# A fused attention block and 7x7 convolution: the stage on v put in a fixed order of thirds, with the edge rows first

## The chip, the core and the metric

The kernel runs on one core of one Trainium2 chip. The metric is the device time of one execution in microseconds, taken as the median of the runs. The core has five engines that run beside each other and wait for one another by semaphores: TensorE (PE, matrix products into PSUM), VectorE (DVE), ScalarE (ACT), GpSimd (POOL) and SyncE (SP, here an issuer of DMAs). ACT, POOL and SP issue DMAs. All data is float32.

## What is computed

Two layers with a residual each, on x of 1 x 384 x 192 x 192. The first is a group norm, a 1x1 convolution to q, k and v, a 2x2 max pool, a 3x3 depthwise convolution, channel attention in 8 heads of 48 channels (four top-k softmaxes, mixed), gelu, doubling to the old size, and a 1x1 projection. The second is a group norm and a 7x7 depthwise convolution with a symmetrised kernel.

```python
# layer 0
qkv = einsum('bchw,oc->bohw', gn(x), w_qkv) + b_qkv
qkv = qkv.reshape(b, 3*c, hs, 2, ws, 2).max(axis=(3, 5))          # 2x2 max pool
qkv = depthwise3x3(qkv, w_dw) + b_dw
q, k, v = split(qkv, 3, axis=1)                                   # each (b, 8, 48, hs*ws)
attn = einsum('bhcn,bhdn->bhcd', unit(q), unit(k)) * temperature  # channel attention
out = sum(topk_softmax(attn, kk) @ v * a for kk, a in ((24, a1), (32, a2), (36, a3), (38, a4)))
out = gelu(out); out = repeat(repeat(out, 2, axis=2), 2, axis=3)
x = x + einsum('bchw,oc->bohw', out, w_proj) + b_proj
# layer 1
w_sym = (w + rot90(w, 1) + rot90(w, 2) + rot90(w, 3)) / 4
x = x + depthwise7x7(gn(x), w_sym)
```

The attention matrix needs q and k of the whole image, and the second group norm needs the whole sum of layer 0. So there are stages: the statistics of x; q and k; the attention matrix; v with attention, projection and residual; and the 7x7 convolution. The sum of layer 0 goes through DRAM (`sd`, and `sh` for the rows that neighbouring strips need) and is read again by the 7x7 stage.

## The kernel before

The 192 image rows are seen as 6 strips of 32 rows (`NT`, `TR`). A block takes the same two rows from each strip, so there are 16 blocks (`NBC`), worked in the order `FIRST, FIRST + 1, ...` modulo 16. Pooling makes one row per strip of a block. Channels are three tiles of 128 (`KT`). A depthwise row needs the pooled rows of the block before, its own and the next; the first two row sets are kept, the others rotate through three.

```python
FIRST = 3
...
    xp2 = dx.enter_context(tc.tile_pool(name="xp2", bufs=4))
    vp = dx.enter_context(tc.tile_pool(name="vp", bufs=5))
    pv = psx.enter_context(tc.tile_pool(name="pv", bufs=2, space=PSUM))
    # the attention matrix: one piece of program, ahead of everything on v
    ...
    for mt in range(KT):                       # rank of every entry among the 48 of its row
        nc.vector.tensor_tensor(gt, other, mine, ALU.is_gt)        # 128 x 2304 each
        nc.vector.tensor_tensor(eq, other, mine, ALU.is_equal)
        nc.vector.tensor_tensor(eq, eq, lower, ALU.mult)
        nc.vector.tensor_tensor(gt, gt, eq, ALU.add)
        nc.vector.tensor_reduce(rank[:, mt, :], gt, AX.X, ALU.add)
    ...
    gp = dx.enter_context(tc.tile_pool(name="gp", bufs=2))
    yp = dx.enter_context(tc.tile_pool(name="yp", bufs=3))
    xrp = dx.enter_context(tc.tile_pool(name="xrp", bufs=2))

    def convolve(i):                           # v before pooling: one block in three thirds
        for t0 in range(0, NT, UT):
            xb = xp2.tile([P, KT, UT, RB * HW], F32, tag="xv")
            for kt in range(KT):
                nc.sync.dma_start(xb[:, kt], image_rows(kt, b, t0, UT))
            for ct in range(KT):
                ps = pv.tile([P, UT, 512], F32, tag="pv")
                # 6 products: ps <- wq, xb                         (L677)
                nc.vector.tensor_reduce(rows[ct][...], ps[...], AX.XY, ALU.max)   # L681

    def depthwise_v(i):                        # 9 taps for each of three channel tiles, L467/L469
        for ct in range(KT):
            taps(vp.tile(...), 2 * KT + ct, win)

    def attend(i, vb):
        for ct in range(KT):
            for h in range(2):
                # 2 or 3 products: ps <- attnT, vb[dt]             (L712)
                nc.scalar.activation(gl[...], ps[:, 0:H], AF.Gelu) # L718

    def project(i, gl):
        for ot in range(KT):
            for h in range(2):
                # 3 products: ps <- wp, gl                         (L731)
                nc.scalar.activation(yh[:, h], ps[:, 0:H], AF.Identity, bias=..., accum_out=ysum[...])
            xr = xrp.tile([P, NT, RB * HW], F32, tag="xr")
            nc.sync.dma_start(xr, image_rows(ot, b, 0, NT))
            for e in range(CP):                # residual add, one column in four at a time, L756
                nc.vector.tensor_tensor(sx[:, v, :, :, dj : dj + NJ], xq[:, :, :, :, e], y[...], ALU.add)
            # two Square activations with accum_out, of 3/4 and 1/4 of sx (L769)
            for a in range(RB):
                nc.gpsimd.dma_start(sdv[r, cs], rows_of(a, CP, 0))            # L783
                # for r < 3 or r >= 29: three more DMAs into sh (halo rows)   # L793

    for i in range(NBC + 3):
        if i - 2 in vbs:  gls[i - 2] = attend(i - 2, vbs.pop(i - 2))
        if i < NBC:       convolve(i)
        if i - 2 in gls:  project(i - 2, gls.pop(i - 2))
        if 0 < i - 1 <= NBC:  vbs[i - 1] = depthwise_v(i - 1)
    ...
    # 7x7 stage: 48 steps of 8 channels; each loads w, main, aux on ACT's queue
    ws = {n: load_w(n) for n in range(2)}
    mains = {n: load_main(n) for n in range(2)}        # main <- sd, aux <- sh
    # group statistics, then rows of mean, std, 1/std over all 384 channels
    for name, v in (("mb", mean1), ("sb", std1), ("rb", rstd1)): along_free(t, v, mps, name)
    for k in range(5): nc.vector.tensor_scalar_mul(mm[:, :, k], mb, mask[:, k : k + 1])
    for n in range(steps): ...                         # 24 products (L1020, L1025, L1031), scaling, stores
```

The scheduler that builds the program may reorder instructions on an engine. `keep_in_program_order` (`keep`) takes this from it; before, only the 7x7 stage used it.

Of the kernel before, what the change touches and what calls it, by code (L numbers as in the profile page):

```python
# [73 lines left out]
FIRST = 3  # L74
# [4 lines left out]
def conv_preact_d2(  # L79
# [169 lines left out]
    st = const.tile([P, KT, NB * SUB, 6], F32, name="st0")  # L249
    mean0 = const.tile([P, KT], F32, name="mean0")  # L250
    rstd0 = const.tile([P, KT], F32, name="rstd0")
    with tc.tile_pool(name="gps0", bufs=1, space=PSUM) as gps:
# [287 lines left out]
    dx = bctx  # L540
    xp2 = dx.enter_context(tc.tile_pool(name="xp2", bufs=4))
    rowp2 = dx.enter_context(tc.tile_pool(name="rowp2", bufs=1))
    vp = dx.enter_context(tc.tile_pool(name="vp", bufs=5))
    pv = psx.enter_context(tc.tile_pool(name="pv", bufs=2, space=PSUM))
    near = {}
    with ExitStack() as ax:
        ap = ax.enter_context(tc.tile_pool(name="ap", bufs=1))
# [4 lines left out]
        nc.vector.reciprocal(rn, rn)  # L552
        tps = ptr.tile([P, C], F32, name="tps", tag="tr")
# [6 lines left out]
        along_free(rkb, rn[:, KT : 2 * KT], ptr, "rk", "tr")  # L560

# [7 lines left out]
        for i, (mt, r0, r1, h) in enumerate(PIECES):  # L569
            eng = (nc.gpsimd, nc.scalar)[i % 2]  # L570
            o = h * HC - SPAN[mt][0]
            eng.dma_start(att[r0:r1, mt, :], scaled[r0:r1, mt, o : o + HC])

# [8 lines left out]
        for mt in range(KT):  # L582
            full = [P, HC, HC]
            other = att[:, mt, :].unsqueeze(1).to_broadcast(full)
            mine = att[:, mt, :].unsqueeze(2).to_broadcast(full)
            gt = ap.tile(full, F32, name=f"gt{mt}", tag="gt")
            eq = ap.tile(full, F32, name=f"eq{mt}", tag="eq")
            nc.vector.tensor_tensor(gt, other, mine, ALU.is_gt)
            nc.vector.tensor_tensor(eq, other, mine, ALU.is_equal)
            nc.vector.tensor_tensor(eq, eq, lower, ALU.mult)  # L590
            nc.vector.tensor_tensor(gt, gt, eq, ALU.add)
            nc.vector.tensor_reduce(rank[:, mt, :], gt, AX.X, ALU.add)

# [5 lines left out]
        nc.scalar.activation(ex, ex, AF.Exp)  # L599
        mix = ap.tile(row3, F32, name="mix")  # L600
        for i, kk in enumerate(KKS):
# [9 lines left out]
            else:  # L611
                nc.vector.tensor_tensor(em, em, rsb, ALU.mult)
                nc.vector.tensor_tensor(mix, mix, em, ALU.add)
        diag = ap.tile([P, KT, C], F32, name="diag")
        nc.gpsimd.memset(diag, 0.0)
        for i, (mt, r0, r1, h) in enumerate(PIECES):
            eng = (nc.gpsimd, nc.scalar)[i % 2]
            eng.dma_start(diag[r0:r1, mt, h * HC : (h + 1) * HC], mix[r0:r1, mt, :])
        for dt in range(KT):
# [13 lines left out]
    bpm = const.tile([P, KT], F32, name="bpm")  # L633
    nc.vector.tensor_tensor(bpm, bp, mean0, ALU.subtract)
    ysum = const.tile([P, KT, NBC, 2], F32, name="ysum")
    sqsum = const.tile([P, KT, NBC, 2], F32, name="sqsum")
    mid1 = const.tile([P, KT], F32, name="mid1")
    negmid = const.tile([P, KT], F32, name="negmid")
    gp = dx.enter_context(tc.tile_pool(name="gp", bufs=2))
    yp = dx.enter_context(tc.tile_pool(name="yp", bufs=3))  # L640
    xrp = dx.enter_context(tc.tile_pool(name="xrp", bufs=2))
    sxp = dx.enter_context(tc.tile_pool(name="sxp", bufs=1))
# [3 lines left out]
    sxs = []  # L646
    for i in range(3):
        t = sxp.tile([P, LEAD + CP * RB * RUN + LEAD], F32, name=f"sx{i}")
        nc.gpsimd.memset(t, 0.0)
        sxs.append(t)  # L650
    H = PBC // 2
    order = [(FIRST + i) % NBC for i in range(NBC)]

# [12 lines left out]
    def convolve(i):  # L666
        b, rows = order[i], place(i)
        for t0 in range(0, NT, UT):
            xb = xp2.tile([P, KT, UT, RB * HW], F32, name=f"xv{b}_{t0}", tag="xv")
            for kt in range(KT):  # L670
                nc.sync.dma_start(xb[:, kt], image_rows(kt, b, t0, UT))
            for ct in range(KT):
                o = (2 * KT + ct) * P
                ps = pv.tile([P, UT, 512], F32, name=f"pv{b}_{t0}_{ct}", tag="pv")
                for u in range(UT):
                    for kt in range(KT):
# [4 lines left out]
                nc.vector.tensor_reduce(  # L681
                    rows[ct][:, 1 + t0 : 1 + t0 + UT, 1 : PS + 1],
                    ps[:, :, 0 : RB * HW].rearrange("p u (a w b) -> p u w a b", a=2, b=2),
                    AX.XY,
                    ALU.max,
                )

    def depthwise_v(i):

        b = order[i % NBC]  # L690
        vb = []
        for ct in range(KT):
            dst = vp.tile([P, NT, PS], F32, name=f"vb{b}_{ct}", tag="vb")

            def win(dy, dx):
                r = b + dy - 1
                t0 = 1 + r // NBC
                return place(i + dy - 1)[ct][:, t0 : t0 + NT, dx : dx + PS]

            taps(dst, 2 * KT + ct, win)  # L700
            vb.append(dst)
        return vb

    def attend(i, vb):
        b = order[i % NBC]
        gl = gp.tile([P, KT, PBC], F32, name=f"gl{b}", tag="gl")
        for ct in range(KT):
            dts = [dt for dt in range(KT) if ct in near[dt]]
            for h in range(2):
                ps = ptr.tile([P, C], F32, name=f"po{b}_{ct}_{h}", tag="tr")  # L710
                for dt in dts:
                    nc.tensor.matmul(  # L712
                        ps[:, 0:H],
                        attnT[:, dt, ct * P : (ct + 1) * P],
                        vb[dt].rearrange("p t c -> p (t c)")[:, h * H : (h + 1) * H],
                        start=(dt == dts[0]), stop=(dt == dts[-1]),
# [6 lines left out]
    def project(i, gl):  # L723
        b = order[i % NBC]
        for ot in range(KT):
            y = yp.tile([P, NT, NJ, 2], F32, name=f"y{b}_{ot}", tag="y")
            yh = y.rearrange("p (h t) j e -> p h (t j e)", h=2)
            for h in range(2):
                ps = ptr.tile([P, C], F32, name=f"pr{b}_{ot}_{h}", tag="tr")
                for ct in range(KT):  # L730
                    nc.tensor.matmul(  # L731
                        ps[:, 0:H],
                        wp[:, ct, ot * P : (ot + 1) * P],
                        gl[:, ct, h * H : (h + 1) * H],
                        start=(ct == 0), stop=(ct == KT - 1),
# [12 lines left out]
            xr = xrp.tile([P, NT, RB * HW], F32, name=f"xr{b}_{ot}", tag="xr")  # L748
            nc.sync.dma_start(xr, image_rows(ot, b, 0, NT))
            flat = sxs[(i * KT + ot) % len(sxs)]  # L750
            body = flat[:, LEAD : LEAD + CP * RB * RUN]
            sx = body.rearrange("p (v a t j) -> p v a t j", v=CP, a=RB, t=NT)
            xq = xr.rearrange("p t (a j e) -> p a t j e", a=RB, e=CP)
            for e in range(CP):
                v, dj = (e + CP - 1) % CP, int(e > 0)
                nc.vector.tensor_tensor(  # L756
                    sx[:, v, :, :, dj : dj + NJ],
                    xq[:, :, :, :, e],
                    y[:, :, :, e // 2].unsqueeze(1).to_broadcast([P, RB, NT, NJ]),
                    ALU.add,  # L760
                )
            runs = body.rearrange("p (n j) -> p n j", j=JP)
            for k, (n0, n1, dj) in enumerate(
                ((0, (CP - 1) * RB * NT, 1), ((CP - 1) * RB * NT, CP * RB * NT, 0))
            ):
                junk = yp.tile(
# [339 lines left out]
```

## Time and profile before

| | before |
|---|---|
| median of 3 runs | 3046.9 us (3043.93 to 3054.62) |
| profiled span | 3052.5 us |
| PE busy | 2697.0 us (88%) |
| DVE busy | 2309.6 us (76%) |
| ACT busy, POOL busy | 787.3 us, 757.3 us |
| DMA | 608.48 MB, mean 199 GB/s |
| first `pv` product (L677) | 1405.4 us |
| first `po` product (L712) | 1551.6 us |
| last `pv` product | 2268.0 us |
| first 7x7 product (L1020) | 2411.6 us |

The costly groups of the stage on v, from the list of groups; the columns are the line, the engine, the operation, what it writes from what, the sizes, the count, then busy time with the mean of one, and the idle time of the engine just before them with what ended most of it:

```profile
L677 PE MATMUL pv<-xv,wq 128*128 128x384 f32 x1728 | 575.2, 493 | 27.0 <-DVE row L681 25.3
L469 DVE SCALAR_TENSOR_TENSOR vb<-row,wd,vb 128x576 f32<-128x576 f32 x384 | 293.1, 811 | 2.1
L681 DVE TENSOR_REDUCE row<-pv 128x192 f32<-128x768 f32 x144 | 137.6, 955 | 187.0 <-PE pv L677 187.0
L756 DVE TENSOR_TENSOR sx<-xr,y 128x576 f32<-128x576 f32 x192 | 218.0, 1200 | 61.5 <-DMA xr<-in_x_dram 54.1
L712 PE MATMUL po<-vb,attnT 128*128 128x288 f32 x448 | 140.7, 456 | 49.7 <-ACT y L737 19.4
```

Durations of neighbours overlap on an engine, because instructions are pipelined. So the time that a group takes is better read from the starts of its instructions than from the sum of their durations.

### The profile page before, as it was taken

To read this page: it belongs to the slowest core of one execution; us is meant where nothing else is said; L and a number is where in the kernel's file an instruction comes from. 1 tells how busy PE (TensorE), PEld (TensorE's weight loads), DVE (VectorE), ACT (ScalarE), POOL (GpSimd) and SP (SyncE) were. 2 spreads that over 40 slices of the span, in tenths; PEclk is the share of its full clock that TensorE was granted. 3 is DMA by queue.
4 is the path that set the end of the run, shared out by engine and by line. 5 is a ranking of instruction groups with operands and counts; after the bars stand their busy time and mean duration, and the time that the engine had idled before them with its cause. 6 is when DMAs were issued, how large, how long until landed. Compare 5 with 4: busy or idle time off the path is not lost.

```text
span 3052.5 us, 25172 instructions
## 1 busy us (share of the span) xinstructions
PE 2697.0 (88%) x8661; PEld 1597.7 (52%) x8661; DVE 2309.6 (76%) x3350; ACT 787.3 (26%) x1497; POOL 757.3 (25%) x878
## 2 busy tenths in 40 slices
PE   0089999999999999999799999999996599989997
PEld 0044444444444444445465555555554477767675
DVE  7957787878787878787867687677677577867775
ACT  0011111111111111112003122122123355666664
POOL 0033444200000000001001000000133367776765
PEclk9999999999999999999999999999997699999999
DMA  9956676401010101002226556556689899999997
GB/s 370 415 179 234 229 243 224 145 31 62 31 62 32 62 31 62 31 1 91 98 93 226 183 170 229 167 187 220 220 265 361 313 345 348 362 362 350 354 354 232
DMA packets 236383, 608.48 MB, mean 199 GB/s; under 512 B 16016, under 2 KB 167472, under 8 KB 220896
## 3 DMA queue, kind: packets, MB, share of 16 engines
q1 hardware_dynamic: 175392, 279.29, 26.7%
q0 software_dynamic: 40256, 161.43, 15.6%
q10 hardware_dynamic: 20608, 166.16, 14.5%
q8 instruction: 69, 1.13, 0.1%
q14 instruction: 58, 0.48, 0.0%
HBM read 385.87 MB, written 220.79 MB: 199 GB/s over the span
## 4 chain that ended last, share of the span: by engine, by line
PE 58%; DMA 19%; DVE 14%; POOL 5%; issue 2%; ACT 1%; ACTq 0%; SPq 0%; POOLq 0%; DVEq 0%
PE pq L417 37%; PE pv L677 12%; DMA main<-sd 6%; DMA out_dram<-res 4%; DVE sx L756 4%; DVE vb L469 4%; DMA xr<-in_x_dram 3%; POOL res L990 2%; DVE st L268 2%; PE grams L496 2%; DMA xs<-in_x_dram 2%; PE tr L487 2%; DMA sh<-sx 1%; PE pc L1031 1%; DVE row L681 1%
## 5 line engine op out<-in xcount | busy, mean ns | idle before, releaser
L417 PE MATMUL pq<-xq,wq 128*128 128x512 f32 x2268 | 990.7, 592 | 0.0
L469 DVE SCALAR_TENSOR_TENSOR qk<-ring,wd,qk 128x384 f32<-128x384 f32 x1152 | 677.4, 613 | 22.5 <-ACT ring L456 7.1
L417 PEld LDWEIGHTS pq<-xq,wq 128*128 128x128 f32 x2268 | 422.9, 190 | 492.2 <-issue 448.7
L677 PE MATMUL pv<-xv,wq 128*128 128x384 f32 x1728 | 575.2, 493 | 27.0 <-DVE row L681 25.3
L424 DVE TENSOR_REDUCE ring<-pq 128x128 f32<-128x512 f32 x432 | 297.4, 688 | 225.8 <-PE pq L417 224.3
L677 PEld LDWEIGHTS pv<-xv,wq 128*128 128x128 f32 x1728 | 331.0, 193 | 259.0 <-DVE row L681 35.5
L1044 DVE TENSOR_SCALAR apart<-pc,rb 32x576 f32<-32x576 f32 x384 | 312.2, 813 | 167.7 <-PE pc L1031 94.9
L1042 ACT ACTIVATE apart<-pc,rb 32x576 f32<-32x576 f32 x384 | 281.4, 733 | 243.3 <-PE pc L1031 111.9
L469 DVE SCALAR_TENSOR_TENSOR vb<-row,wd,vb 128x576 f32<-128x576 f32 x384 | 293.1, 811 | 2.1
L1031 PE MATMUL pc<-aux,w 128*128 128x288 f32 x768 | 255.9, 415 | 41.9 <-POOL main L929 19.6
L681 DVE TENSOR_REDUCE row<-pv 128x192 f32<-128x768 f32 x144 | 137.6, 955 | 187.0 <-PE pv L677 187.0
L756 DVE TENSOR_TENSOR sx<-xr,y 128x576 f32<-128x576 f32 x192 | 218.0, 1200 | 61.5 <-DMA xr<-in_x_dram 54.1
L1020 PE MATMUL pc<-main,w 128*128 128x288 f32 x768 | 256.4, 416 | 4.6 <-POOL main L929 3.1
L1025 PE MATMUL pc<-main,w 128*128 128x288 f32 x768 | 254.6, 413 | 0.0
L783 POOL DMA_DIRECT2D sd<-sx x96 | 72.3, 756 | 640.1 <-DVE sx L756 429.6
L990 POOL COPY res<-apart 128x1152 f32<-128x1152 f32 x96 | 220.9, 2330 | 23.7 <-ACT apart L1042 20.8
L478 ACT ACTIVATE junk<-qk 128x384 f32<-128x384 f32 x144 | 75.3, 523 | 575.9 <-DVE qk L469 575.9
L576 POOL MEMSET lower<- 128x2304 f32 x1 | 2.0, 2019 | 850.8 <-PE grams L496 850.8
L1031 PEld LDWEIGHTS pc<-aux,w 128*128 128x128 f32 x768 | 147.4, 194 | 89.9 <-POOL main L929 26.5
L712 PE MATMUL po<-vb,attnT 128*128 128x288 f32 x448 | 140.7, 456 | 49.7 <-ACT y L737 19.4
L1020 PEld LDWEIGHTS pc<-main,w 128*128 128x128 f32 x768 | 148.0, 194 | 49.8 <-PE pc L1031 3.6
L1025 PEld LDWEIGHTS pc<-main,w 128*128 128x128 f32 x768 | 149.0, 194 | 43.6
(170 smaller groups left out, 2270.0 us busy)
## 6 DMA issues: line engine op xcount, KB each, us to landing
w<-wt ACTq DMA_DIRECT2D x48, 1536.0 KB, 9.2
sd<-sx POOLq DMA_DIRECT2D x96, 600.0 KB, 9.8
main<-sd ACTq DMA_DIRECT2D x48, 1200.0 KB, 9.8
xv<-in_x_dram SPq DMA_DIRECT2D x144, 384.0 KB, 4.3
xr<-in_x_dram SPq DMA_DIRECT2D x48, 1152.0 KB, 11.1
out_dram<-res SPq DMA_DIRECT2D x192, 288.0 KB, 7.5
xs<-in_x_dram SPq DMA_DIRECT2D x23, 2304.0 KB, 11.5
xq<-in_x_dram SPq DMA_DIRECT2D x21, 2304.0 KB, 8.9
```

The lines of the kernel that those rows point to most:

```text
L417: nc.tensor.matmul(ps, wq[:, kt, ct * P : (ct + 1) * P], rows[:, kt, :, g * 64 : (g + 1) * 64], start=(kt == 0), stop=(kt == KT - 1),)
L424: nc.vector.tensor_reduce(t[:, r0 : r0 + PR, 1 + g * 32 : 1 + (g + 1) * 32], ps.rearrange("p (h a w b) -> p h w a b", h=PR, a=2, b=2), AX. ...
L469: nc.vector.scalar_tensor_tensor(dst, src, w, dst, ALU.mult, ALU.add)
L677: nc.tensor.matmul(ps[:, u, 0 : RB * HW], wq[:, kt, o : o + P], xb[:, kt, u, :], start=(kt == 0), stop=(kt == KT - 1),)
L681: nc.vector.tensor_reduce(rows[ct][:, 1 + t0 : 1 + t0 + UT, 1 : PS + 1], ps[:, :, 0 : RB * HW].rearrange("p u (a w b) -> p u w a b", a=2, ...
L756: nc.vector.tensor_tensor(sx[:, v, :, :, dj : dj + NJ], xq[:, :, :, :, e], y[:, :, :, e // 2].unsqueeze(1).to_broadcast([P, RB, NT, NJ]), ...
L990: keep(nc.gpsimd.tensor_copy(res[:, k], apart[:, :, k].rearrange("p e n -> p n e")))
L1020: nc.tensor.matmul(acc, w[:, i, 0:P], main[:, i, :, 0:NJ], start=True, stop=False)
L1025: nc.tensor.matmul(acc, w[:, i, P : 2 * P], main[:, i, :, 1 : 1 + NJ], start=False, stop=False,)
L1031: nc.tensor.matmul(acc, w[:, i, 2 * P :], aux[:, i, :, 0:NJ], start=False, stop=True,)
L1042: keep(nc.scalar.mul(dst, src, scale))
L1044: keep(nc.vector.tensor_scalar_mul(dst, src, scale))
```

## The change

It reorders the stage on v, and moves work between its beginning and its end. What it is for:

- TensorE's order in the blocks is fixed: a third of a convolution, the attention products of the block two behind, a third, the projection, a third. Between a product and what it waits for there is other work.
- The depthwise rows are begun as soon as two of the three input rows are there, and ended when the third comes. Three blocks are convolved beside the computation of the attention matrix, which is handed out in small pieces between thirds.
- The order of blocks begins at 13 in place of 3, so the blocks that write halo rows (14, 15, 0, 1) are attended first, not last.
- One pool of six x buffers serves the convolution and the residual; the residual is added two columns at a time, for four instructions as before.
- The first two steps' loads of the 7x7 stage are issued on SP's queue, from memory that comes free before the stage ends. The channel rows are made for the first 128 channels only, and for the others within later steps.

```diff
-FIRST = 3
+FIRST = NBC - 3
...
-    xp2 = dx.enter_context(tc.tile_pool(name="xp2", bufs=4))
-    vp = dx.enter_context(tc.tile_pool(name="vp", bufs=5))
+    xp2 = dx.enter_context(tc.tile_pool(name="xp2", bufs=6))
+    vp = dx.enter_context(tc.tile_pool(name="vp", bufs=6))
...
+    def attention(ap):              # the old code with a yield after each larger step
...
+    AHEAD = 3
+        chain = attention(ap)
+        for i in range(AHEAD):
+            for t0 in range(0, NT, UT):
+                convolve(i, t0, lambda ins: ins)
+                for _ in range(3):
+                    next(chain, None)
+            if i == AHEAD - 1:
+                for ct in range(KT):
+                    depthwise_v(1, ct, (0, 1))
...
-    gp = dx.enter_context(tc.tile_pool(name="gp", bufs=2))
+    gp = dx.enter_context(tc.tile_pool(name="gp", bufs=1))
-    xrp = dx.enter_context(tc.tile_pool(name="xrp", bufs=2))
...
     # attend: halves outside, channel tiles inside; products of attend and project under keep(...)
-        for ct in range(KT):
-            for h in range(2):
+        for h in range(2):
+            for ct in range(KT):
...
-            xr = xrp.tile([P, NT, RB * HW], F32, name=f"xr{b}_{ot}", tag="xr")
+            xr = xp2.tile([P, NT, RB * HW], F32, name=f"xr{b}_{ot}", tag="xv")
...
-            for e in range(CP):
-                nc.vector.tensor_tensor(
-                    sx[:, v, :, :, dj : dj + NJ], xq[:, :, :, :, e],
-                    y[:, :, :, e // 2].unsqueeze(1).to_broadcast([P, RB, NT, NJ]), ALU.add)
+            for k, e in enumerate((2, 0)):
+                for a in range(RB):
+                    nc.vector.tensor_tensor(
+                        bass.AP(flat.tensor, flat.offset + at(e, a),
+                            [flat.ap[0], [JP, NT], [1, NJ], [at(e + 1, a) - at(e, a), 2]]),
+                        xq[:, a, :, :, e : e + 2],
+                        y[:, :, :, e // 2].unsqueeze(3).to_broadcast([P, NT, NJ, 2]), ALU.add)
+                # one Square of 2 x 576 after each pair, its output in the unused part of wq
...
-    for i in range(NBC + 3):
-        if i - 2 in vbs:
-            gls[i - 2] = attend(i - 2, vbs.pop(i - 2))
-        if i < NBC:
-            convolve(i)
-        if i - 2 in gls:
-            project(i - 2, gls.pop(i - 2))
-        if 0 < i - 1 <= NBC:
-            vbs[i - 1] = depthwise_v(i - 1)
+    for i in range(AHEAD, NBC + 3):
+        j = i - 2
+        if i < NBC:
+            convolve(i, 0, keep)
+        for ct in range(KT):
+            depthwise_v(j, ct, (last_row(j),))
+        gl = attend(j)
+        if i < NBC:
+            convolve(i, UT, keep)
+            for ct in range(KT):
+                depthwise_v(i - 1, ct, (0, 1))
+            ...                     # rows of the last two blocks that are known already
+        ys = project(j, gl)
+        if i < NBC:
+            convolve(i, 2 * UT, keep)
+        residual(j, ys)
...
     # 7x7 stage
+    def queue(n):
+        if n < 2:
+            return nc.sync.dma_start
+        return lambda dst, src: keep(nc.scalar.dma_start(dst, src))
...
-        for name, v in (("mb", mean1), ("sb", std1), ("rb", rstd1)): along_free(...)   # 384 channels
+        along(mb, mean1, 0)(); masked(0); along(sb, std1, 0)(); middle(0); ... along(rb, rstd1, 0)()
+            if 1 < n < KT + 1:      # within steps 2 and 3
+                done = [along(d, v, n - 1) for d, v in ((mb, mean1), (sb, std1), (rb, rstd1))]
+                ...
+                masked(n - 1)
```

## The prediction

> **What bounds the kernel now.** I read the slices of the span first, then windows over the stages, then TensorE's time line in one block, then single waits. The slices (76 us each) show four stages: statistics to about 165 us, the convolution of q and k to about 1430, the stage on v to 2411, where the first 7x7 product starts, and the 7x7 stage.
>
> ```profile
> PE 0089999999999999999799999999996599989997
> DVE  7957787878787878787867687677677577867775
> PEclk9999999999999999999999999999997699999999
> DMA  9956676401010101002226556556689899999997
> ```
>
> TensorE (PE) is nearly full on v, and drops to 6 and 5 in two slices around 2300 to 2440 us, with its clock. The DMA engines are half idle for most of v and full from there on. The windows say more. Columns: busy time and count of PE, weight loads, VectorE (DVE), ScalarE (ACT), GpSimd (POOL); granted clock; DMA share; GB/s. The rows are one steady block of v, the last block with convolutions, the tail in three parts, and the 7x7 stage.
>
> ```profile
> 1678.00:1734.00 56.00, 51.77 (x173) 32.26 (x172) 41.08 (x49) 12.98 (x30) 4.49 (x6) 1.00 0.58 192
> 2216.00:2275.00 59.00, 56.12 (x186) 35.64 (x185) 44.02 (x52) 14.18 (x35) 17.86 (x24) 0.97 0.84 279
> 2275.00:2330.00 55.00, 40.33 (x140) 28.44 (x138) 48.16 (x59) 23.63 (x56) 22.36 (x30) 0.91 0.98 334
> 2330.00:2378.00 48.00, 22.97 (x75) 16.46 (x75) 26.32 (x35) 16.54 (x38) 11.21 (x15) 0.66 0.98 337
> 2378.00:2412.00 34.00, 9.64 (x36) 8.12 (x36) 19.19 (x49) 8.20 (x13) 6.79 (x14) 0.50 0.89 330
> 2440.00:3052.00 612.00, 556.41 (x2213) 425.63 (x2211) 441.62 (x460) 368.40 (x418) 429.15 (x407) 0.96 0.96 338
> ```
>
> So there are three limits: TensorE in a steady block (VectorE has 41 of 56 us), DMA in the tail of v and in the 7x7 stage (0.96 to 0.98, at 334 to 338 GB/s). Inside a block TensorE's time line shows where it is not at work; the brackets give the idle time and who ended it.
>
> ```profile
> 1670.18 35.27 PE L677 MATMUL pv<-xv,wq 128*128 128x384 f32 x108
> 1705.28 8.89 PE L731 MATMUL pr<-gl,wp 128*128 128x288 f32 x36
> 1714.01 1.13 PE L712 MATMUL po<-vb,attnT 128*128 128x288 f32 x4
> 1716.24 2.48 PE L712 MATMUL po<-vb,attnT 128*128 128x288 f32 x8 [1.09 <-ACT y L737]
> 1719.75 0.75 PE L712 MATMUL po<-vb,attnT 128*128 128x288 f32 x2 [1.04 <-DVE vb L469]
> 1721.24 3.66 PE L712 MATMUL po<-vb,attnT 128*128 128x288 f32 x14 [0.74 <-ACT gl L718]
> 1724.74 7.90 PE L677 MATMUL pv<-xv,wq 128*128 128x384 f32 x24
> 1734.32 27.36 PE L677 MATMUL pv<-xv,wq 128*128 128x384 f32 x84 [1.68 <-DVE row L681]
> ```
>
> All the small waits come where `po` follows `pr` at once: `po` needs PSUM that `pr`'s readers still hold, and a depthwise row (`vb`) that VectorE has not finished. (A product of the program is two records here: 108, 36 and 28 in a block.)
>
> [...] an L731 record lasts 0.406 us, yet 36 take 8.7 us, 0.24 each; so I work with start-to-start times. [...] The old residual add reads x in steps of 16 bytes and takes 1.14 us for 576 elements, while the rank comparisons take 2.55 us for 2304, that is 0.64 for 576. The new add reads pairs, but scatters its writes; no run here shows that form, so I count no gain.
>
> **Part 1: TensorE's order in the steady blocks.** The least time of a block, start to start: `pv` 34.9 us (2233.47 to 2268.34), `pr` 8.7 (1705.28 to 1714.01), `po` 28 x 0.25 = 7.0 (14 records in 3.66). Sum 50.6. A block now takes 56.2 (`pr` at 1705.28 and at 1761.52). So 5.6 us a block is waits. The change puts a third of the convolution (11.6 us) between each pair of dependent steps: `po` waits for its last depthwise row behind one third, `pr` for the gelu behind the next, and the third after `pr` covers the y reads and the residual. In the changed program as built, VectorE takes the reduction of a tile, three taps, the next reduction, and so on, and the last row of a block is done when the second tile of the third is reduced. I give it 1.5 us a block of remaining waits: 4 us x 13 blocks = 52 us gained.
>
> **Part 2: the attention phase.** VectorE's rank comparisons now hold up the reductions of `pv`: TensorE idles 3.8, 4.5, 4.9, 4.6 and 1.5 us between 1428 and 1508, 19 in all. The new order has one comparison (2.55) and one reduction (0.95) per tile, 3.5 us against the 3.87 that a `pv` tile takes on TensorE. So about 12 of the 19 go. Depthwise work is pulled in here too, and VectorE gets nearly full; the first `po` might wait a little.
>
> **Part 3: the edge rows and the tail.** The halo stores (`sh`) are 36 x 600 KB and 18 x 300 KB, 27.6 MB, all after 2163 us, 83 us of DMA at 334 GB/s. They sit in the tail, where a residual load takes 18 us to land instead of 10.5, and the last adds wait for it 8 us apiece. From the last `pv` (2268) to the first `pc` (2411) are 143 us. With the edges first, what follows the last `pv`: TensorE 3 x (7.0 + 8.7) = 47 us; VectorE some 22 taps at 0.75 = 17 and three residuals of 12 x 1.14 = 41, so 58 plus a few us of waiting; DMA about 13 MB of stores, 7 of x, 7 of first 7x7 loads, 27 MB or 80 us at 335 GB/s, partly begun earlier. Then the statistics, which took 18 us from the last add (2393) to the first product. I take 62 + 18 and 5 for the DMA: 85 us, so 58 gained.
>
> **Part 4: what it costs.** The halos now fall into the first four attended blocks. A steady block moves 10.7 MB; a full edge block adds 6 x 1.5 MB, 19.9 MB in all, 59 us at 335 GB/s against a block of 52, for two blocks; the two half edges (15.3 MB, 46 us) fit. The window 2216 to 2275 had such stores beside a block of 56 us at 0.84 without slowing it, and six x buffers cover most of a block. I charge 10 us.
>
> **Part 5: the 7x7 stage.** 48 steps of 4.49 MB at 338 GB/s are unchanged. The earlier loads and the split of the channel rows (one third of them now, two inside steps) may save 3 us at the start.
>
> Sum: 52 + 12 + 58 - 10 + 3 = 115, which gives 3046.9 - 115 = 2932. As a check from the other end: `pv` from 1405, 16 x 34.9 = 558, 13 x 15.7 = 204, the rest of q/k 16, waits 7 + 20 + 10: last `pv` at 2220, first `pc` at 2305, then 641 us as now, less 3: 2943 of span, and the median lies 5.6 below the profiled span: 2937. I say 2935.
>
> **Rivals.** (a) VectorE takes TensorE's place. It has 42 us of work in a block of 52, and in the new order ten residual adds stand in one run ahead of the reduction of the last third: 11.4 us, starting 4 us after `pr` (8.7) begins, so that reduction comes about 3 us late, just what two PSUM buffers absorb. If the new add took 1.5 us instead of 1.14, TensorE would lose 3 to 5 us a block and the gain of part 1 would be gone: about 2985. For it: the scattered writes. Against it: the paired reads. (b) The halo stores at the front stop VectorE's in-order queue (three sx buffers, not read out yet), and so TensorE: up to 15 us in each of two blocks, about 2955. (c) The tail was DMA bound anyway, and with 27 MB still to move it stays at 110 us: about 2960. Speaking for it is the 0.98; against it that 28 MB of the old tail are gone. (d) All waits vanish and the pair reads speed the adds to 0.8 us, which shortens VectorE's tail by 12 us: about 2900.
>
> **Range and chances.** The parts are waits seen in the trace, and the two large ones are independent, so it takes failures in both to lose the gain. Range 2895 to 2985. Two per cent is 61 us, half of the sum. Faster by over 2%: 0.89; within 2%: 0.09; slower: 0.02.
>
> **What would show it.** Right: blocks of 51 to 53 us between successive `pr`; `po` no longer led by waits for y; `sh` stores at 1600 to 1800 us; last `pv` near 2220 and first `pc` near 2305; a 7x7 stage of about 640. Wrong: blocks at 56 with waits of `pv` for `row` (rival a), first edge blocks over 60 (b), DMA at 0.98 and over 100 us after the last `pv` (c). A longer 7x7 stage would upset the sum from a side that I count as untouched.

## The result, and the profile after

The changed kernel takes 2952.6 us (median of four runs, 2945.4 to 2954.0) against 3046.0 for the kernel before, measured beside it. The ratio is 0.968, with a 95% interval of 0.966 to 0.971: 3.2% faster. The prediction said 2935, between 2895 and 2985.

The profiled execution is 102 us shorter than that of before (2950.5 against 3052.5 us). Four marks on TensorE split it:

| stretch | before, us | after, us | difference | predicted |
|---|---|---|---|---|
| start to first `po` (attention phase) | 1551.6 | 1535.7 | -15.9 | -12 |
| first `po` to last `pv` (blocks) | 716.4 | 672.2 | -44.2 | -52 + 10 |
| last `pv` to first `pc` (tail) | 143.6 | 99.2 | -44.4 | -58 |
| first `pc` to the end (7x7 stage) | 640.9 | 643.4 | +2.5 | -3 |

The marks don't cut the same work in both kernels. In the changed one 360 `pv` records stand ahead of the first `po` and not 324 (one third more, 11.6 us), and 108 `pr` records behind the last `pv` and not 144 (one projection less, 8.7 us). For equal work of TensorE the first three differences are some -28, -41 and -36 us, an estimate from these times.

The page of after, the same rows of its slices (74 us each now):

```profile
PE   0089999999999999999999999999997799989987
...
DMA  9956677201101010100437996657566899999997
```

TensorE has no 6 and 5 any more where v ends, only two sevens. The DMA row shows 9 and 9 at the front of the stage on v: there the halo copies are now. Windows of after, with the columns of the prediction's table: one block, the tail from 2240 us in three parts, the 7x7 stage.

```profile
1922.70:1975.40 52.70, 51.06 (x174) 32.52 (x173) 40.44 (x48) 13.66 (x30) 4.49 (x6) 1.00 0.61 205
...
2240.00:2270.00 30.00, 25.54 (x97) 17.56 (x97) 17.62 (x16) 18.51 (x44) 7.49 (x10) 1.00 0.88 312
2270.00:2290.00 20.00, 5.05 (x26) 4.12 (x25) 14.28 (x32) 9.54 (x18) 5.14 (x10) 0.64 0.54 183
2290.00:2307.00 17.00, 5.12 (x19) 4.17 (x19) 5.32 (x20) 0.00 (x0) 1.15 (x2) 0.50 1.01 412
2340.00:2950.00 610.00, 552.45 (x2206) 422.61 (x2205) 443.23 (x472) 364.67 (x413) 428.75 (x402) 0.97 0.95 338
```

The tail is bound by DMA no longer: its share is 0.54 just ahead of the end and then 1.01 for the last 17 us. So something is loaded late that could have come in the half idle 20 us before. TensorE's time line in a block:

```profile
1911.08 11.77 PE L679 MATMUL pv<-xv,wq 128*128 128x384 f32 x36
1922.69 8.89 PE L782 MATMUL pr<-gl,wp 128*128 128x288 f32 x36
1931.42 7.91 PE L679 MATMUL pv<-xv,wq 128*128 128x384 f32 x24
1940.91 16.23 PE L679 MATMUL pv<-xv,wq 128*128 128x384 f32 x48 [1.59 <-DVE row L684]
...
1975.38 8.89 PE L782 MATMUL pr<-gl,wp 128*128 128x288 f32 x36
```

From `pr` to `pr` it is 52.69 us (56.2 before). The four waits of before are one of 1.59 us, in the third after `pr`: two of its three tiles run, and the next finds both PSUM buffers still unread. VectorE's time line in the same block says why:

```profile
1926.42 2.37 DVE L817 TENSOR_TENSOR sx<-xr,y 128x576 f32<-128x576 f32 x2 [2.58 <-ACT y L789]
1930.27 4.25 DVE L817 TENSOR_TENSOR sx<-xr,y 128x576 f32<-128x576 f32 x4 [1.48 <-ACT wq L826]
1935.45 4.63 DVE L817 TENSOR_TENSOR sx<-xr,y 128x576 f32<-128x576 f32 x4 [0.93 <-ACT y L789]
1939.91 0.94 DVE L684 TENSOR_REDUCE row<-pv 128x192 f32<-128x768 f32 x1
```

Ten residual adds stand ahead of the reduction, and TensorE goes on when that has ended (1940.9). That is the run of adds that rival (a) named. It costs 1.6 us and not 3 to 5.

The work left to VectorE after the last `pv` is next: first the kernel before, 2268 to 2412, then the changed one, 2208 to 2307. In such group lines the last number is the idle time ahead of the group, with what ended it.

```profile
L756 DVE TENSOR_TENSOR sx<-xr,y 128x576 f32<-128x576 f32 x48 | 53.9, 1184 | 33.6 <-DMA xr<-in_x_dram 26.3 <-ACT y L737 4.4 <-ACT gl L718 2.9
L469 DVE SCALAR_TENSOR_TENSOR vb<-row,wd,vb 128x576 f32<-128x576 f32 x46 | 34.6, 805 | 0.1
...
L467 DVE TENSOR_SCALAR vb<-row,wd,bdb 128x576 f32<-128x576 f32 x4 | 2.3, 584 | 0.0
```

```profile
L817 DVE TENSOR_TENSOR sx<-xr,y 128x576 f32<-128x576 f32 x37 | 41.4, 1173 | 19.2 <-ACT wq L826 11.8 <-ACT y L789 6.2 <-ACT gl L767 0.8
L711 DVE SCALAR_TENSOR_TENSOR vb<-row,wd,vb 128x576 f32<-128x576 f32 x24 | 17.9, 825 | 0.0
```

Taps 50 to 24, adds 48 to 37, and 26.3 us of waits for the loads of x are gone: 90.8 us of work and 33.7 of waits became 59.3 and 19.2. Eleven of the adds are not saved: they stand ahead of the last `pv` now. New is a wait of 11.8 us for line 826, ScalarE's Square over the sums. In each channel tile two adds, a Square, two adds and a second Square stand in the source; in the program as built the third add waits for the first Square, though the two touch different planes. Their bounding ranges in `sx` overlap, which may be why; no run tests that.

The end of the tail is a load. A line of SyncE's queue waits from 2230 to 2310 (who waited, for what, us in all, times, the longest), then the chain of work that ended last:

```profile
SPq L927 <- DVE part L955: 28.1, 1, 28.1
```

```profile
2288.04 0.57 SPq L937
...
2290.34 16.23 DMA main<-sd
```

The 7x7's first weights and auxiliary planes (L927, L937) were meant to lie beside the end of v. Their memory overlaps the x buffers of the last residual, so they are issued at 2287 to 2289, after the last add, and the first `main` (the planes themselves), behind them on the same queue, lands only at 2306.6 (2290.34 and 16.23).

### The profile page after: what moved, and what is told of

The parts are those of the page before. It is cut to its first block, busy times and chain, and to the rows that moved or that the text cites. A ratio compares the mean times of both kernels' runs of the same rounds, so it can differ in the third digit from the quotient of the medians.

```text
span 2950.5 us, 25225 instructions
## 1 busy us (share of the span) xinstructions
PE 2663.8 (90%) x8661; PEld 1586.9 (54%) x8661; DVE 2294.8 (78%) x3354; ACT 794.5 (27%) x1497; POOL 763.4 (26%) x878
## 4 chain that ended last, share of the span: by engine, by line
PE 67%; DMA 13%; DVE 12%; POOL 4%; ACT 2%; issue 2%; ACTq 0%; SPq 0%; POOLq 0%; DVEq 0%
PE pq L420 38%; PE pv L679 11%; DVE sx L817 5%; DMA out_dram<-res 3%; PE pc L1139 3%; PE pc L1128 3%; PE pc L1133 3%; DMA main<-sd 3%; DMA sh<-sx 3%; PE po L760 3%; DVE st L271 2%; PE grams L499 2%; DVE vb L711 2%; DMA xs<-in_x_dram 2%; POOL res L1099 2%; PE tr L490 2%
## 5 line engine op out<-in xcount | busy, mean ns | idle before, releaser
L826 ACT ACTIVATE wq<-sx,negmid 128x1152 f32<-128x1152 f32 x96 | 120.5, 1255 | 158.8 <-DVE sx L817 154.4
```

## The experiments

Theory T: the blocks gained from the order of TensorE's work in thirds, the tail from the halos' move; what stayed long in the tail is the Square between adds and the late first loads, and in the block VectorE's run of adds. Rival R: the thirds matter little, and the tail is paced by the chain `po`, Gelu, `pr`, y of some 20 us a block or by its bytes.

The kernels ran on several chips, each beside the kernel before; the ratio to it is what may be compared. Us are that difference from the changed kernel's 0.9684, times 3047. The interval of 0.9684 alone is 7 us to each side, so a difference of some 8 us or less is not clear of noise.

| run | ratio to before, 95% | to the changed kernel, us |
|---|---|---|
| a_again | 0.9688 (0.9671 to 0.9705) | +1 |
| e1_squares_last | 0.9694 (0.9679 to 0.9709) | +3 |
| e6_loads_beside | 0.9666 (0.9649 to 0.9684) | -5 |
| e9_adds_apart | 0.9646 (0.9629 to 0.9663) | -12 |
| e12_apart_later | 0.9618 (0.9605 to 0.9632) | -20 |
| e2_edges_last | 0.9744 (0.9715 to 0.9772) | +18 |
| e3_only_edges_first | 0.9969 (0.9955 to 0.9982) | (-9 from before) |
| e4_free_order | 0.9672 (0.9642 to 0.9702) | -4 |
| e5_attention_first | 0.9739 (0.9710 to 0.9768) | +17 |
| e10_whole_blocks | 0.9709 (0.9695 to 0.9722) | +8 |
| e11_late_taps | 0.9705 (0.9692 to 0.9719) | +6 |
| e13_add_forms | one run, 2920.4 us, against 3047.4 | about -31 |

### The changed kernel again, as the yardstick

> The changed kernel itself, so that the three beside it are compared on the same chip. Both theories: about 2950 us, last pv matmul to first pc matmul 99 us, a block of the middle 52.7 us with one wait of 1.6 us at pv.

Measured: tail 99.8 us, a block of the middle 52.7, 2963.6 us on a chip where the kernel before takes 3059.3. As expected, but for that chip, which is slower by 0.4% for both kernels, and for two blocks with halo copies, which take 57.0 and 55.6 us.

### Squares after all adds

```
     for k, e in enumerate((2, 0)):
         for a in range(RB): nc.vector.tensor_tensor(...)
+    for k, e in enumerate((2, 0)):
         nc.scalar.activation(junk, ..., AF.Square, ...)
```

> The two Squares of a channel tile stand after its four adds instead of two adds, Square, two adds, Square. Theory (the adds of the tail wait for ScalarE's Square, 3.0 + 1.5 + 3.0 + 2.9 us of waits on line 826 after the last pv): the waits on Square ahead of the third add of a tile go, the last add ends 5 to 8 us sooner, the total falls by 6 to 10 us; the wait of 1.6 us per block in the middle stays within 0.4 us. Rival (the tail is paced by the chain po, Gelu, pr, y of about 20.4 us per block on TensorE and ScalarE, or by its bytes): the adds then wait for y instead, the total falls by no more than 3 us.

Measured: in the tail the theory holds, the waits for line 826 are gone and last `pv` to first `pc` takes 91.8 us against 99.8; about half of these waits turned into waits for y (13.0 us in place of 6.2). But the total didn't fall, because the last `pv` came 9 us later. Of twelve blocks nine take 54.4 us and three 52.7, with a wait of 1.9 to 2.1 us in each. One of either kind:

```profile
1949.93 17.44 PE L679 MATMUL pv<-xv,wq 128*128 128x384 f32 x48 [2.05 <-DVE row L684]
...
2058.66 15.79 PE L679 MATMUL pv<-xv,wq 128*128 128x384 f32 x48 [2.05 <-DVE row L684]
```

Without the Squares between them all twelve adds run through, and the scheduler put the reduction behind all twelve. The wait grew from 1.59 to 2.05 us, yet most blocks grew by 1.7: there the 48 records after the wait take 17.44 us, and 15.79 in the others. Windows of TensorE after this wait in four successive blocks (the clock is third from the end) show why:

```profile
1896.40:1899.70 3.30, 3.30 (x7) 0.50 1.04 407
1951.00:1954.30 3.30, 3.30 (x7) 0.50 1.04 404
2005.60:2008.90 3.30, 3.30 (x6) 0.50 1.03 403
2060.20:2063.50 3.30, 3.30 (x12) 1.00 1.06 403
```

The clock is 0.50 through the 3.3 us of the window in three of the four, with 6 or 7 records in it, and 1.00 in the last, with 12, after the same wait. After the 1.59 us in the blocks of the changed kernel it stays 1.00 throughout (1551 to 2200 us). What sets the fourth block apart, no run shows. So a wait of 1.9 to 2.1 us was followed by a loss of another 1.7 us in nine blocks and by none in three.

### The first 7x7 loads really beside the stage

```
-  auxp, wtp(3), wide, mainp(3), outp
+  auxp, mainp(3), wide, a gap of 2560 floats, wtp(3), outp
```

> The buffers of the 7x7's first weights and auxiliary planes lie over memory of the v stage that comes free before the last adds (row sets and depthwise outputs) and no longer over the x buffers of the last residual; nothing else is changed. Theory (the first loads came late because their memory was held until the last add, issued at 2287 with the queues at half load from 2260 to 2290): weights and the first auxiliary planes are issued by 2250 to 2265, the first pc starts 5 to 8 us sooner, the total falls by 7 to 12 us. Rival (the tail's bytes bind in any case, loads moved forward only delay the stores of planes and the halo): 0 to 3 us.

Measured: the first weights now wait for TensorE's `po` and not for the last add, the DMA share from 2260 to 2290 is 0.88 against 0.68 in the changed kernel on that chip, `main` lands in 12.3 us in place of 16.5, and the first `pc` comes 5.0 us sooner after the last `pv`. The total is 5.5 us lower on that chip; the intervals overlap, and 7 to 12 were expected. In the two profiles the 7x7 stage is 4.5 us longer (648.1 against 643.6), and of the whole span only 1.9 us are left. So the tail follows the theory, and a gain of the total is not shown. Only the weights moved: the auxiliary planes still wait for what comes after the last add, and `main` stands behind them on SyncE's queue.

```profile
SPq L939 <- DVE part L957: 27.2, 1, 27.2
```

### Adds in two fixed lots

```
-  residual(j, ys) after the last third
+  adds of channel tiles 0 and 1, in fixed order
+  reduction of the last third's first tile, in fixed order
+  adds of channel tile 2, then the other reductions
   (with the edits of the two runs above)
```

> Holds the edits of the two runs before, and beside them the twelve adds of a block are put in VectorE's fixed order in two lots: eight ahead of the reduction of the first channel tile of the last third, four after it. Theory (the one wait of 1.58 us left in a block is the pv of the third whose PSUM buffer waits for a reduction that stands behind all twelve adds, 12 x 1.1 us): the wait goes to under 0.3 us, a block takes 51.1 us against 52.7, and the total falls by 25 to 35 us, of which 16 come from the blocks. Rival (VectorE is only moved: the next reduction now stands behind four adds and TensorE waits there as long): a block stays within 0.3 us of 52.7 and the total falls by what the two edits give, 10 to 18 us.

Measured: a block takes 51.2 us, as the theory said, and the wait of `pv` is 0.6.

```profile
1959.17 11.88 PE L679 MATMUL pv<-xv,wq 128*128 128x384 f32 x36 [0.61 <-DVE row L685]
```

The total fell by 13 us on that chip, half of what was expected. At the `pr` where the steady blocks begin it was 11 us behind (1784.6 against 1773.3 in the changed kernel on that chip): 3.5 us already at the first `pv`, most of the others in the blocks with halo copies, where `pv` waits 18.0 us from 1540 to 1820 (3.8 of it for x) against 11.4.

### The same, with VectorE left free in the edge blocks

```
+  if 5 <= j and i < NBC:   the two fixed lots
+  else:                    order as in the changed kernel
```

> As the run with the twelve adds in two lots of fixed order, but the order is fixed only from the sixth attended block on, so that VectorE is free in the blocks with halo copies, where that run lost 8 us to waits of pv for its row reduction and for x. Theory (in the edge blocks adds in a fixed place hold VectorE until a halo store has read its sx buffer): steady blocks of 51.2 us as there, the edge blocks as in the changed kernel, the total 18 to 26 us below the changed kernel. Rival (those 8 us come from the changed places of the 7x7 buffers or from the loads of x): the same total as that run, 10 to 14 us below the changed kernel.

Measured: 2930.4 us, ratio 0.9618, some 20 us below the changed kernel and 8 us below the run with fixed lots everywhere. The size is the theory's: a block 51.2 us, the edge blocks 52.7 to 54.4, the last `pv` at 2197.1, the tail 87.0. The theory's reason doesn't show. In the slowest edge block of the run with fixed lots (66.8 us) the adds wait 6.5 us for a load of x and not for a halo store. That load took 37 us to land:

```profile
1707.27 37.26 DMA xr<-in_x_dram
```

The changed kernel's repeat has such a load too, in the block of 55.6 us (41.8 us to land); in the block of 57.0 ahead of it the adds do wait for a halo store, 2.9 us. In the changed kernel's steady blocks these loads land in 12 us. Since the changed kernel itself loses 0 to 7 us in the edge blocks from one profile to the other, how much of the 8 us is due to the free order stays open. It is the best kernel of this study that computes the whole reference: 3.8% faster than before.

### Edges last again, and edges first alone

```
-FIRST = NBC - 3      (in the changed kernel)
+FIRST = 3
```

> The changed kernel with the edge row blocks at the end of the loop again (FIRST = 3), all else of the change kept. Theory (the halo copies and their late stores were a large part of the old tail of 143.6 us): last pv to first pc grows from 99 to 125 to 145 us, the total rises by 25 to 45 us against the changed kernel. Rival (the shorter tail comes from early depthwise taps and shared buffers, not from where the edges stand): the tail grows by no more than 5 us.

```
-FIRST = 3            (in the kernel before)
+FIRST = NBC - 3
```

> The kernel before with one constant changed: FIRST = NBC - 3, so that the edge row blocks stand in the first blocks; nothing else of the change. Theory: the tail of the kernel before shrinks from 143.6 to about 110 us and the total falls by about 30 us against before. Rival (halo copies among the first blocks, where GpSimd and the queues are used by the attention phase and its blocks of 56 us, make those blocks longer by as much): the total stays within 5 us of before.

Measured: with the edges last the tail is 118.1 us (+19), the total 18 to 21 us higher; the last `pv` does not move (2210.3). The chain shows how, halo store after halo store:

```profile
2203.96 15.59 DMA sh<-sx
...
2219.83 15.14 DMA sh<-sx
```

In the kernel before, edges first alone shorten the tail from 143.6 to 128.2 us, and the total by 7 to 9 only, less than the 30 of the theory. The rival's loss in the front is there too, but small: the last `pv` is 3 us later (2271.1, on another chip), with a `pv` wait of 4.8 us in a block with halos, where VectorE waits 5.8 us for a load of x. So the halos' place is worth 15 to 19 us in the tail. The other 25 to 29 go with VectorE's shorter list: that kernel still has 50 taps and 48 adds after the last `pv`, against 24 and 37, some 32 us of work; eleven of the adds and a projection (8.7 us) are only moved ahead. No run takes the list alone.

### Does the fixing matter? Do the thirds?

```
-keep = tc.keep_in_program_order      (v stage only)
+keep = lambda ins: ins
```

> The changed kernel without the fixed program order on TensorE's instructions of the v stage: the compiler's scheduler orders them, and in the program as built it arrives at nearly the same thirds. Theory (the fixing itself carries the gain in the blocks): blocks go back to about 56 us and the total rises by about 40 us. Rival (that the source emits thirds and begins the depthwise row by row is enough, the fixing is only a guard): the total stays within 5 us of the changed kernel.

```
-  third, attend(j), third, project(j, gl), third
+  attend(j), third, third, third, project(j, gl)
   (all in fixed order, so po follows pr at once)
```

> The changed kernel with the three thirds of a row block's convolution put together again on TensorE: po, then 108 pv records, then pr, and po of the next block at once after pr, as before; taps begun row by row, shared buffers and edge order stay. Theory (the thirds between dependent steps carry the gain in the blocks): a block goes back from 52.7 to 55.5 to 56.5 us, with waits of po for y and of pr for the Gelu, and the total rises by 40 to 55 us against the changed kernel. Rival (the last depthwise row, done early, was what po waited for; y and Gelu cost little): a block of 53 to 54.5 us, the total rises by 5 to 25 us.

Measured: without the fixing 2956.9 us, the same time, with the same 1.58 us wait in a block: the rival is right. With whole blocks the total is 8 us higher, with overlapping intervals, and the block doesn't change: from the second `pv` stretch at 1916.08 to the next at 1968.82 it is 52.74 us.

```profile
1943.27 8.89 PE L782 MATMUL pr<-gl,wp 128*128 128x288 f32 x36
1952.06 3.66 PE L760 MATMUL po<-vb,attnT 128*128 128x288 f32 x14
1956.57 1.24 PE L760 MATMUL po<-vb,attnT 128*128 128x288 f32 x4 [0.85 <-ACT gl L767]
1958.11 2.69 PE L760 MATMUL po<-vb,attnT 128*128 128x288 f32 x10 [0.30 <-ACT gl L767]
...
1968.82 16.39 PE L679 MATMUL pv<-xv,wq 128*128 128x384 f32 x50 [0.28 <-DVE row L684]
```

Here `po` follows `pr` as before, and of the old waits only 0.85 and 0.30 for the Gelu and 0.28 for the reduction are left. None for `vb`, none for y. The theory of the thirds, on which Part 1 was built, falls, and the rival's block of 53 to 54.5 isn't met either. The thirds trade these 1.4 us for the one wait of 1.59. The 8 us, if they are real, lie outside the steady blocks. The tail of 106.8 us doesn't show them, for it holds the projection (8.7 us) that the changed kernel has ahead of the last `pv`.

### Attention first

```
     chain = attention(ap)
+    for _ in chain: pass
     for i in range(AHEAD): ...
```

> The changed kernel with the attention's chain of VectorE work emitted whole ahead of the first three blocks, as before, instead of three pieces after each third. Theory (three comparisons between two reductions are what TensorE waited for, 4.5 to 4.9 us each): three or so such waits come back among the first blocks, the first po starts 10 to 15 us later and the total rises by 10 to 14 us. Rival (the attention chain's end, and not the pv matmuls, sets the first po): within 3 us of the changed kernel.

Measured: 17 to 21 us more; the first `po` 21.5 us later (1557.2), where 10 to 15 were expected. All `pv` records from 1400 to 1560, of the changed kernel and of this one:

```profile
L679 PE MATMUL pv<-xv,wq 128*128 128x384 f32 x396 | 130.9, 489 | 1.7 <-DMA xv<-in_x_dram 1.7
```

```profile
L679 PE MATMUL pv<-xv,wq 128*128 128x384 f32 x360 | 127.2, 512 | 13.1 <-DVE row L684 11.7 <-DMA xv<-in_x_dram 1.4
```

Three waits of 3.5 to 4.5 us came back (11.4 us more idling), and each is followed by slow matmuls: the granted clock is 0.57, 0.63 and 0.66 in the first 7, 7 and 5 us after them. The 24 records after one of 3.77 us take 10.58 us instead of 7.9. 360 records at 23 ns more are 8 us: 11 + 8 = 19 of the 21.5.

### Taps of the last blocks late

```
-            if NBC - 6 <= i < NBC - 3: depthwise_v(NBC, ..., (1, 2))
-            if NBC - 3 <= i < NBC:     depthwise_v(NBC - 1, ..., (2,))
-            if i == NBC - 1:           depthwise_v(NBC - 1, ct, (0,))
+    last_row(i): (2, 0, 1) for NBC - 1, (1, 2, 0) for NBC
```

> The changed kernel without the early taps of the last two row blocks in the loop's order: their 36 taps that the change lays into the six blocks before stand in the tail again. Theory (VectorE paces the tail, so that taps moved ahead shorten it by their own time): 36 x 0.64 to 0.75 us = 23 to 27 us, the tail grows from 99 to 118 to 126 us and the total rises by 18 to 27 us. Rival (a tail block is paced by the chain po, Gelu, pr, y of some 20 us on TensorE and ScalarE, and the taps lie beside it): the total rises by no more than 8 us.

Measured: 6 us more, within the intervals' overlap, and a tail of 99.6 us, as without the edit. The run does not decide what it was made for: VectorE has the same 24 taps after the last `pv`, so in the program as built the scheduler had drawn the taps forward by itself. What lets it do so would be their buffers (own `vlast` buffers and six `vb` in place of five in all), which the edit left; that was not tried.

### Forms of the add

```
   tile 0: pairs of x, sums scattered into two planes (as changed)
   tile 1: pairs of x, sums side by side
   tile 2: x contiguous, sums side by side
```

> A look at the residual add (576 f32 elements, 1.09 us start to start, no faster for reading x in pairs of 8 bytes). One channel tile keeps the add of the change; the second writes its sums to neighbouring places instead of two scattered planes; the third reads x contiguously as well. This leaves out the right placement of the sums of two channel tiles; the amount of work is the same. Theory A (the scattered writes set the time): the second form takes about 0.64 to 0.75 us, as 576 elements of the rank comparisons did, the third no less. Theory B (reads of x in pairs set it): the second stays at 1.09, the third falls to 0.64 to 0.75. Theory C (neither; y read twice per element, or the add itself): all three within 5%.

The sums of two channel tiles land in wrong places here, with the same count of elements; it is one run. The three forms from 1450 to 2400 us, in the order tile 0, 2, 1:

```profile
L827 DVE TENSOR_TENSOR sx<-xr,y 128x576 f32<-128x576 f32 x64 | 75.0, 1172 | 61.7 <-ACT y L789 35.0 <-ACT wq L834 22.1 <-DMA sd<-sx 4.1
L833 DVE TENSOR_TENSOR sx<-xr,y 128x576 f32<-128x576 f32 x64 | 46.8, 753 | 17.7 <-ACT y L789 9.2 <-ACT wq L834 6.2 <-DMA xr<-in_x_dram 2.2
L829 DVE TENSOR_TENSOR sx<-xr,y 128x576 f32<-128x576 f32 x64 | 46.7, 749 | 0.0
```

Theory A: scattered writes cost 0.42 us an add (1172 to 749 ns), contiguous reads nothing more (753). A block's adds get 3.4 us shorter, and the block falls to 50.7 us (`pr` at 1913.28 and 1963.96), the 50.6 that the prediction worked out as the least; `pv` waits for a reduction only 1.3 us in the whole stage. So the one wait of 1.59 us is VectorE's add time.

## Why the prediction was right, point by point

**What bounds it.** Right in the blocks: TensorE with waits, VectorE at 40 of 52.7 us. DMA as the limit of the tail held only as long as the halos were there: its share is 1.03 from 2210 to 2270 us with the edges last, and 0.65 to 0.80 in the tail of before with the edges first.

**Part 1, the blocks: size nearly right, reason wrong.** 4 us times 13 was to be 52; with 56.2 to 52.7 it is 3.5 times 13 = 46 (41 between the marks, for equal work). The step "the change puts a third of the convolution between each pair of dependent steps" is not what removed the waits: whole blocks have 52.74. What they share with the changed kernel, and not with before, are taps begun row by row, the larger set of `vb`, six shared x buffers, halves of `po` outermost and paired adds. The order of the row blocks is not it: 52.7 us in the changed kernel with the edges last, some 56 in before with the edges first. In the kernel before, the chain of every second block runs from the load of x for the last residual over its adds to the reduction that `pv` waits for; in the others it runs over adds, Squares and Gelu to `po`. In the changed kernel that load is waited for no longer: from 1550 to 2200 us the adds of before wait 25.1 us for x, and those of the changed kernel for y (36.9 us), Squares (17.7) and stores (5.1). The chain of work of before, in one block of the first kind:

```profile
1826.10 9.27 DMA xr<-in_x_dram
1835.49 4.56 DVE sx L756 x4
...
1842.11 3.64 DVE vb L469 x5
1845.75 0.88 DVE row L681
...
1846.68 19.63 PE pv L677 x60
```

The load of x for the last residual sets when the adds end, these when the taps and the reduction, and so when `pv` goes on. Which of these carries how much stays open; they were not tried one by one.

"So 5.6 us a block is waits" is not quite what the trace has. The waits of the block shown in the prediction sum to 4.5 us, and those of every second block to some 2.8. The next block is one of these, with its clock (third from the end) in the second view:

```profile
1772.47 2.48 PE L712 MATMUL po<-vb,attnT 128*128 128x288 f32 x8 [1.09 <-ACT y L737]
1775.96 0.75 PE L712 MATMUL po<-vb,attnT 128*128 128x288 f32 x2 [1.01 <-DVE vb L469]
1777.45 5.35 PE L712 MATMUL po<-vb,attnT 128*128 128x288 f32 x14 [0.74 <-ACT gl L718]
```

```profile
1778.30:1781.60 3.30, 3.30 (x8) 0.50 1.03 354
```

After the same three waits the clock falls to 0.50 here, and the 14 records take 5.35 us and not 3.66. But this block has no wait of `pv`, and takes 56.1 us against 56.2. That both come out alike speaks for a pace set by the chain above and not by the sum of TensorE's waits.

**Part 2, the attention phase: right, too small.** 16 us gained against 12, some 28 for equal work, and 21.5 lost when undone. With whole blocks, where the work ahead of the first `po` is that of before, it comes 23 us earlier (1528.3). Three of the five waits, 4.5, 4.9 and 4.6 us, were `pv` waiting for a reduction, and are gone. The 3.8 us belong to a product of the attention itself, which waits for VectorE, and are 3.81 in both kernels. The prediction counted the waits and left out the clock: it had read 1.00 in steady blocks and 0.5 in the tail, but not that it falls after single waits (to 0.57 to 0.66 over 5 to 7 us with attention first).

**Part 3, the tail: right direction, 14 us too much.** 8.7 us of the 58 are no gain: they are the projection moved ahead of the last `pv`, and the sum charges them nowhere. "62 + 18 and 5": the last add ended 79.5 us after the last `pv`, not 62. VectorE's work was sized right (58 against 59.3 us busy), the waits were not: "a few us" were 19, of them 11.8 for the Square, which the prediction did not see in the built program. Taking them away gave 8 us in the tail. The 18 became 20, the first loads at the end of it worth 5. Of the 44 gained, the halos, which the part put first, account for 15 to 19; the greater part goes with VectorE's shorter list, part of which is only moved. That the list carries it is argued: the run that was to show it left the taps where they were.

**Part 4, the cost: 0 to 7 us in place of 10.** In the profile of after three blocks with halos take 158.0 us (`pr` at 1606.6 and 1764.7), 52.7 each like the others; in the repeat on another chip they take 165.3. Parts 1 and 4 together were 42 us and came to 44, by luck: two errors that cancel.

**Part 5: wrong, small.** "The earlier loads" did not come earlier, and the stage is 2.5 us longer instead of 3 shorter.

**Rivals.** (a) is there at 1.6 us a block. The add kept its old cost (1.09 us against 1.14), it seems because the two reasons given cancelled: with sums side by side in both, the old add, which reads x in steps of 16 bytes, takes 1200 ns and the paired one 749, and scattering takes the 0.42 us back. The two read y differently as well, so the share of x is not isolated. (b) is absent from the profile of after, but not from the kernel: in the repeat two edge blocks take 57.0 and 55.6 us, with a `pv` wait of 3.5 and 3.3; it is larger (66.8) where VectorE's order was fixed. (c) is wrong for the changed kernel, whose DMA share is 0.54 to 0.88 until its last 17 us. (d) describes what is possible: without scattered writes 2920.

The sum of 115 us was 102 in the profiles; in the medians it is 93, because before's profiled execution took 8.2 us more than its median and after's 0.4 less.

## What to carry to other kernels

When several waits sit side by side where two steps meet, look for what they have in common upstream (a buffer count that holds back a load or a row of taps) before crediting an order that would hide them: a run that only restores the order tells the two apart. Compare two stretches only after counting the work in each: a product moved over a mark looks like a gain. For a tail, list what each engine has to do after the last big product and read the waits in the program as built. A place in memory decides when a "prefetch" starts (here at 2287 us, after the last add), and an add into one plane may wait for a reader of another (11.8 us in this tail). Fix an engine's order only where nothing irregular can hold it up, such as the load that took 37 us to land beside halo stores.

## What was not expected of the hardware

- TensorE's waits of 1.6 us left the clock at 1.00 in the changed kernel. A wait of 2.05 us was followed by a clock of 0.50 over a window of 3.3 us in three blocks of one run, at 1.7 us more, and by 1.00 in a fourth; three waits of 0.7 to 1.1 us in `po` were followed by 0.50 over 3.3 us in one block of before (14 records in 5.35 us) and not in another (3.66 us). After those of 3.5 to 4.5 us the clock was 0.57 to 0.66 over 5 to 7 us, and the three cost some 8 us together. What decides whether the clock falls, no run shows.
- An add of 576 f32 whose result goes to two planes 4 bytes at a time takes 1172 ns, with side by side results 749 ns; reads of x in pairs of 8 bytes or contiguous make no difference (749 and 753). The cost is in the scattered writes, 0.42 us an add, which the prediction had left open.
- Halo stores of about 15 us each beside the first blocks, at a DMA share of 0.87 from 1540 to 1740 us, cost a stage with six x buffers nothing in one profile and 7 us in another, where a residual's load of x took 41.8 us to land.
